# Three more tiles turned by VectorE, gather slots cleared later, result adds and scatters later, in a masked-attention kernel

## The chip, the cores and the metric

The kernel runs on one core of a Trainium2 chip. The metric is the device time of one execution in microseconds (us). Engines: PE is TensorE (matmuls), ACT is ScalarE, DVE is VectorE, POOL is GpSimd, SP is SyncE (it only issues transfers here). Each engine works through its own queue in order; what it issues to the DMA queues runs beside it.

## The reference

The inputs are x (2708 rows of 1024 numbers), a sparse 0/1 matrix adj (2708 x 2708, about four ones to a row), and three weight matrices with biases. What is computed:

```
h = max(layernorm(x), 0)
q, k, v = h @ Wq.T + bq,  h @ Wk.T + bk,  h @ Wv.T + bv
z = (q @ k.T) / 32 * adj;  zeros of z become -10000
out = x + relu(softmax(z, axis=1) @ v)
```

## The kernel before

All numbers are 32-bit floats. The rows are 22 tiles of 128 (the last has 20 rows). Because adj is so sparse, the kernel never forms q @ k.T. It multiplies Wq and Wk into one matrix M, searches each row of adj for its ones, sorts the rows by their number of ones (two separate sorts, of the first 8 tiles and of the rest), and then, for each row, gathers only the rows of h that it needs.

**Start.** Up to about 104 us PE forms M, while x is normalised and stored to `h_dram`. The search on DVE (line 389) goes on to 199 us. The second sort, of the first 8 tiles, ends with `pos_i` (line 689). POOL then *puts* (line 626) the list of each row into a table in memory at its sorted place, and the table is loaded back (`reload`). From then on POOL can gather.

**Units.** From 106 us PE works through 20 units of two tiles each, numbered n = 0 to 19, and then one single tile. Units 0 to 9 ("q") multiply pairs of h tiles by M. Units 10 to 19 ("o") multiply pairs of attention sums by Wv. The pairs of the last units are 18 = (14, 1), 19 = (16, 9); the single tile is 8. A unit is a two-by-two block product done with seven blocks of eight matmuls instead of eight blocks (Winograd's form), so sums and differences of operands (line 722, on DVE) go in, and sums of results (lines 1091, 1094, 1121, 1125 or 1152, 1156) come out. `multiply` (from line 1044) walks through a unit in seven steps i = 0 to 6, calling `after(i)` at each, where everything else is placed. The first two blocks of the next unit (`between`, `opened`) run ahead of the last block of this one; for unit 19 the single tile's first block (`one_started`) takes that place.

**Turning.** A block needs its left operand transposed. There are two ways. *Turned* (`half_turned`, line 415): PE transposes 128 x 128 pieces against an identity matrix, eight to a tile, and ACT copies them out of PSUM (line 718, or 422 for the single tile). *Faced* (lines 695 to 706 and 942 to 946): ACT copies the finished sums `u` into another order `v` (line 944) and stores them to `u_dram` (line 946); four loads (`by_quarters`, line 700, issued by SP) bring the tile back with its 32 x 32 squares in their places; DVE transposes within the squares (`faces`, line 705). The upper half of the next unit's operands is made at step 0, the lower half at step 2. Of the o tiles, those of units 10 to 14 are faced. The later ones are turned; seven of those, the last pair and the single one among them, stay in SBUF (`held`) and go to PE directly.

**The stream.** From unit 4 on, the attention itself runs on DVE as one stream of steps, tile after tile in the list `order`, which ends with 14, 1, 16, 9, 8: *scores* (line 863, one op for each gathered row), *weights* (lines 906 to 912) and *sums* (lines 923 and 929). `advance(share)` at each step of a unit lets as much of the stream into DVE's queue as `share` (line 1233) allows, 20.9 us a unit, less 2.3 for each faced tile of the next unit. DVE keeps this written order. POOL gathers rows of h into 11 slots (line 610). A gather leaves out the lists' empty places, so the slots are cleared once beforehand: eight on DVE (line 1254, in program order at step 1 of unit 4) and three on POOL in quarters (line 1304, behind the counts of the sort).

**Results.** In an o unit, ACT writes relu of the four results into `ya` and `yb` (lines 1118, 1122, 1126, 1134), four such buffers in all. POOL then adds the rows of x to each by an accumulating gather (`add_x`, line 1109), and scatters the previous one to the output (`scatter`, line 808). The last unit (`ends`, line 1140) gathers its x rows beforehand (line 612), and DVE adds (line 1146). The last tile of 20 rows, all equal, is made from one row (`tail`, line 1175) during unit 14.

Of the kernel before, what the change touches and what calls it, by code (L numbers as in the profile page):

```python
# [18 lines left out]
P = 128  # L19
# [46 lines left out]
def tile_preln_masked_attention(  # L66
# [852 lines left out]
    def sums(t):  # L919
        u, coef, m = us.pop(t)  # L920
        for s in range(0 if t in EMPTY else 1, K[t]):
            fill()
            chained(lambda: nc.vector.scalar_tensor_tensor(  # L923
                u, g_of[t][s], coef[:, s:s + 1], u, op0=ALU.mult, op1=ALU.add))
            free.append(g_of[t][s])
            yield 1.3
        fill()
        if t in HOSTS:
            chained(lambda: nc.vector.scalar_tensor_tensor(
                u[:HP], g_of[t][K[t]][:HP], m[:HP, 3:4], u[:HP], op0=ALU.mult, op1=ALU.add))  # L930
            free.append(g_of[t][K[t]])
            yield 1.3
            fill()
        g_of.pop(t)
        if t == SECOND:
            nc.sync.dma_start(v_dram, u)
            whole_second.append(True)
            return
        unit = next((n for n, pair in enumerate(units) if pair[0] == "o" and t in pair[1:]), len(units))
        if now < [unit - 2, 2] and unit <= len(q_pairs) + 4:  # L940
            faced_tiles.add(t)
        if t in faced_tiles:
            v = row_tile(f"v_{t}")
            nc.scalar.copy(v.rearrange("p (a c r) -> p c a r", a=QUADS, r=QP),
                           u.rearrange("p (c a r) -> p c a r", a=QUADS, r=QP))
            nc.scalar.dma_start(u_dram[t * P:(t + 1) * P, :], v)
        elif near(t):
            held[t] = u
        else:
            nc.sync.dma_start(u_dram[t * P:(t + 1) * P, :], u)  # L950
        done.add(t)
# [159 lines left out]
    def o_results(ta, tb):  # L1111
        ya = work.tile([P, D], FT, tag="q", name=f"y_{ta}", bufs=4)
        yb = work.tile([P, D], FT, tag="q", name=f"y_{tb}", bufs=4)
        if (ta, tb) == o_pairs[-1]:
            return ends(ya, ta, yb, tb)

        def c11(X):
            nc.scalar.activation(ya[:, lo], X, AF.Relu)

        def c22(Y, p5):  # L1120
            nc.vector.tensor_add(p5, copied(Y), p5)
            nc.scalar.activation(yb[:, hi], p5, AF.Relu)

        def c12(Z, u2):
            nc.vector.tensor_add(u2, Z, u2)
            nc.scalar.activation(ya[:, hi], u2, AF.Relu)
            if ta == NT - 2:

                nc.sync.dma_start(tail_dram, ya[P - 1:, :])
            send(add_x(ya, ta))  # L1130
            sent.append((ya, ta))

        def c21(Y):
            nc.scalar.activation(yb[:, lo], Y, AF.Relu)  # L1134
            send(add_x(yb, tb))
            sent.append((yb, tb))

        return c11, c22, c12, c21

# [23 lines left out]

        return c11, c22, c12, c21

    sent = []

    def send(behind):

        while sent:  # L1170
            y, t = sent.pop(0)
            with tc.issue_after(behind.ins):
                scatter(y, t, P)

    def tail(t):
        n = tiles[t][1]
        y = work.tile([P, D], FT, tag="q", name=f"y_{t}", bufs=4)
        nc.sync.dma_start(y[:n], tail_dram.to_broadcast([n, D]))
        add_x(y, t, n)
        scatter(y, t, n)  # L1180

    def of_wv(i, j):

# [41 lines left out]
    for n, unit in enumerate(units):  # L1225
# [4 lines left out]
            ordered.enter_context(tc.manual_schedule(engines={mybir.EngineType.DVE}))  # L1230
            nc.sync.dma_start(bp_dram, bp_sb[0:1, :])
        turn = n in (0, FIRST - 1)
        share = 20.9 / 7
        nxt = units[n + 1] if n + 1 < len(units) else None
        if nxt is not None and nxt[0] == "o":
            share -= 2.3 / 7 * len(set(nxt[1:]) & faced_tiles)
# [1 line left out]

        def after(i):
            now[1] = i  # L1240
            if (n, i) in steps_ahead:
                follow(steps_ahead[n, i])
            if (n, i) == (2, 5):
                owe(8)
                owe(9)
                rows_of[FIRST] = load_rows(units[FIRST])
                owe(10)
                owe(6)
                owe(7)
                rows_of[FIRST + 1] = load_rows(units[FIRST + 1])  # L1250
                pooled.close()
            if (n, i) == (FIRST, 1):
                for g in slots[:HIGH - 3]:
                    nc.vector.memset(g, 0.0)
            b11, b12, b21, b22 = M[:, 0, 0], M[:, 0, 1], M[:, 1, 0], M[:, 1, 1]
            for at, place, src in (((-1, 0), b12, of_wv(0, 1)), ((0, 0), b11, of_wv(0, 0)), ((0, 2), T[:, 1], of_wv(1, 1)),
                                   ((0, 3), b21, of_wv(1, 0)), ((0, 4), b22, of_wv(1, 1))):
                if (n - last_q, i) == at:
                    nc.sync.dma_start(place, src)
            for at, place, a, b in (((0, 2), T[:, 0], b12, b11), ((0, 4), T[:, 1], T[:, 1], T[:, 0]),  # L1260
                                    ((1, 0), T[:, 2], b22, b12), ((1, 1), T[:, 3], b21, T[:, 1])):
                if (n - last_q, i) == at:
                    nc.vector.tensor_sub(place, a, b)
            if (n - last_q, i) == (1, 1):
                free.extend(M.rearrange("p i j (a c) w -> p i j a (c w)", a=2)[:, 0, 1, a, :] for a in range(2))
            if (n, i) == (FIRST, 5):
                next(stream)
            if (n, i) == (FIRST, 6):
                chain.append(behind[-1])
                next(stream)  # L1270
                nc.vector.tensor_tensor(bad, bad, total, op=ALU.not_equal)
            if (n, i) == (FIRST + 1, 6):
                marked(EARLY, NT)
            if (n, i) == (FIRST + 2, 4):
                nc.vector.tensor_scalar(msq, msq, MLIMIT, None, op0=ALU.is_gt)
            if n > FIRST + 1 or n == FIRST + 1 and i > 1:
                advance(share)
            if nxt is not None:

                if i == (3 if n == 0 else 4 if turn else 0):  # L1280
                    ops_of[n + 1] = blocks(*rows_of[n + 1], nc.gpsimd if n + 1 < FIRST - 1 else None)
                    with tc.issue_after(products[-1].ins) if n + 1 == FIRST else nullcontext():
                        ops_of[n + 1][1]()
                if i == (4 if n == 0 else 5 if turn else 2):
                    ops_of[n + 1][2]()
                    rows_of.pop(n + 1)
                    if n == last_q - 1:
                        all_rows()
                if i == 3:
                    banks_of[n + 1] = banks_for(bp_sb)  # L1290
                if i == 6 and n + 2 < FIRST:
                    natural_rows(n + 2)
                if i == (2 if n in (FIRST, last_q) else 4) and n + 2 > FIRST and n + 2 < len(units) and n + 2 not in rows_of:
                    while units[n + 2][0] == "o" and not done.issuperset(units[n + 2][1:]):
                        advance(1.0)
                    rows_of[n + 2] = load_rows(units[n + 2])
            if (n, i) in steps_at:
                follow(steps_at[n, i])
            if (n, i) == (3, 4):
                searched()  # L1300
            if (n, i) == (3, 5):
                for s in range(8, HIGH):
                    for c in range(0, D, D // 4):
                        clear = nc.gpsimd.memset(slots[s][:, c:c + D // 4], 0.0)
                        tc.add_manual_dep(clear.ins, counted_at[-1].ins.name,
                                          mybir.DependencyInfo(mybir.DependencyClass.Sync, mybir.DependencyReason.DATA),
                                          reason="not beside the counts")
            if i == 3 and units[n - 1][0] == "o" and NT - 2 in units[n - 1][1:]:
                tail(NT - 1)
            if nxt is None and i == 1:  # L1310
                while alone not in done:
                    advance(1.0)
                r, = load_rows(("o", alone))
                single["turned"] = turned(r, "alone")
            if nxt is None and i == 3:
                single["banks"] = banks_for(bp_sb)
            if n == last_q - 1 and i == 4:

                nc.sync.dma_start(bp_sb, bv.to_broadcast([P, D]))
            if (n, i) == (last_q, 1):  # L1320
                nc.vector.tensor_sub(bp_sb[:, NB:], bp_sb[:, NB:], bp_sb[:, :NB])
# [233 lines left out]
```

## Time and profile before

| what | value |
|---|---|
| median of 3 runs | 639.91 us (639.73 to 640.34) |
| the profiled execution | 639.94 us |
| its span, first to last instruction | 638.1 us |
| PE clock granted | 0.997 of full speed |
| PE, DVE, ACT, POOL busy | 98%, 82%, 44%, 56% of the span |
| memory moved by DMA | 176.96 MB, mean 277 GB/s |

The span is what the trace covers; 1.84 us of the execution lie around it. A matmul's recorded duration reaches past the start of the next one, so the cost of an item on PE is read from start to start. "Idle before, releaser" in a row says how long the engine stood before it and what ended that.

### The profile page before, as it was taken

How to read it: one execution, taken by the hardware profiler on the slowest of the kernel's cores; microseconds unless marked ns; L12 is line 12 of the kernel's file. 1: busy time of each engine (PE TensorE's matmuls, PEld its weight loads, DVE VectorE, ACT ScalarE, POOL GpSimd, SP SyncE). 2: the span in 40 equal slices, each digit the busy share in tenths (PEclk: the TensorE clock that was granted, in tenths of full speed). 3: DMA queues.
4: the chain of work that ended last, by engine and by line, in shares of the span. 5: the costliest groups of instructions: out<-in, count | busy, mean ns of one | idle time of the engine just before them, and what ended most of it. 6: DMA issues, size and time to landing. Idle time of an engine off the chain costs nothing.

```text
span 638.1 us, 6156 instructions
## 1 busy us (share of the span) xinstructions
PE 627.8 (98%) x1651; PEld 317.9 (50%) x1651; DVE 522.4 (82%) x1016; ACT 283.6 (44%) x423; POOL 360.2 (56%) x383
## 2 busy tenths in 40 slices
PE   9999999999999999999999999999999999999994
PEld 5777766444444444444444444444444444444441
DVE  5999888997997625999888999999999889989121
ACT  3538985849667533424342144343342432333200
POOL 2639960885768357565651663476466878633311
PEclk9999999999999999999999999999999999999998
DMA  8999997598796439996798998999999999853631
GB/s 335 407 362 321 342 351 286 200 323 330 255 379 231 171 95 317 327 323 223 233 299 289 290 414 222 295 344 311 363 382 325 325 290 291 266 145 77 187 119 50
DMA packets 60192, 176.96 MB, mean 277 GB/s; under 512 B 9799, under 2 KB 15255, under 8 KB 59512
## 3 DMA queue, kind: packets, MB, share of 16 engines
q0 software_dynamic: 25136, 78.41, 39.4%
q1 hardware_dynamic: 29514, 78.61, 35.0%
q10 hardware_dynamic: 5502, 19.48, 7.8%
q8 instruction: 15, 0.25, 0.2%
q14 instruction: 25, 0.20, 0.1%
HBM read 145.65 MB, written 40.74 MB: 292 GB/s over the span
## 4 chain that ended last, share of the span: by engine, by line
PE 90%; issue 4%; POOL 2%; DMA 2%; DVE 1%; POOLq 0%; ACT 0%; ACTq 0%; DVEq 0%
PE ps L1010 40%; PE psy L1010 29%; PE ps_y L476 6%; PE ps_x L476 4%; PE ps_z L476 4%; PE pt L415 4%; POOL g L610 2%; DMA v_dram<-u 1%; DMA M<-h_dram,tab 1%; PE ps_y L511 1%; DVE junk L863 0%; PE ps_h L1218 0%; PE ps_v L594 0%; DVE u L923 0%; DVE s L722 0%
## 5 line engine op out<-in xcount | busy, mean ns | idle before, releaser
L610 POOL DMA_INDIRECT g<-h_dram,tab x94 | 120.2, 1278 | 79.9 <-DVE u L923 30.0
L1010 PE MATMUL psy<-wlow,s 128*128 128x512 f32 x320 | 144.0, 592 | 0.0
L1010 PE MATMUL ps<-M,a 128*128 128x512 f32 x320 | 144.0, 593 | 0.0
L863 DVE SCALAR_TENSOR_TENSOR junk<-g,pq 128x1024 uint8<-128x1024 f32 x93 | 113.8, 1224 | 13.4 <-DMA g<-h_dram,tab 10.4
L1010 PEld LDWEIGHTS ps<-M,a 128*128 128x128 f32 x320 | 59.7, 190 | 70.4 <-issue 69.1
L923 DVE SCALAR_TENSOR_TENSOR u<-g,coef,u 128x1024 f32<-128x1024 f32 x69 | 88.4, 1281 | 7.0 <-ACT u L912 5.8
L1010 PEld LDWEIGHTS psy<-wlow,s 128*128 128x128 f32 x320 | 59.6, 190 | 69.2 <-issue 69.0
L389 DVE FIND_INDEX8 at<-ones,adj 128x8 uint32<-128x685 f32 (+1 forms) x88 | 74.5, 864 | 0.0
L1010 PE MATMUL ps<-wlow,s 128*128 128x512 f32 x160 | 72.0, 593 | 0.4 <-DVE s L722 0.4
L1010 PE MATMUL ps<-M,s 128*128 128x512 f32 x160 | 72.1, 592 | 0.0
L1010 PE MATMUL psy<-wlow,a 128*128 128x512 f32 x160 | 72.0, 593 | 0.0
L368 ACT ACTIVATE sized<-adj 128x2708 uint8<-128x2708 f32 (+1 forms) x22 | 54.3, 2467 | 7.4 <-DMA adj<-in_adj_dram 6.1
L298 POOL TENSOR_TENSOR hsum<-hsum,x 128x256 f32<-128x256 f32 (+1 forms) x56 | 38.6, 732 | 26.2 <-DVE wlow L444 22.5
L1109 POOL DMA_INDIRECT y<-in_x_dram,tab x19 | 34.2, 1798 | 28.9 <-ACT y L1134 12.1
L1010 PEld LDWEIGHTS ps<-wlow,s 128*128 128x128 f32 x160 | 30.3, 190 | 38.9 <-issue 38.5
L1010 PEld LDWEIGHTS psy<-wlow,a 128*128 128x128 f32 x160 | 30.3, 190 | 38.5 <-issue 37.3
L1010 PEld LDWEIGHTS ps<-M,s 128*128 128x128 f32 x160 | 30.3, 190 | 38.1 <-issue 37.4
L808 POOL DMA_INDIRECT out_dram<-y,tab x21 | 27.4, 1306 | 32.0 <-DMA y<-in_x_dram,tab 15.8
L912 ACT ACTIVATE u<-g,coef 128x1024 f32<-128x1024 f32 x18 | 20.7, 1149 | 35.8 <-DVE coef L911 35.6
L276 ACT ACTIVATE x<-x,r 128x1024 f32<-128x1024 f32 (+1 forms) x22 | 25.9, 1232 | 6.6 <-POOL r L266 6.6
L722 DVE TENSOR_TENSOR s<-a,pt 128x512 f32<-128x512 f32 x30 | 19.2, 681 | 10.9 <-ACT a L718 10.9
L476 PE MATMUL ps_y<-wlow 128*128 128x512 f32 x64 | 27.6, 592 | 0.0
(251 smaller groups left out, 843.3 us busy)
## 6 DMA issues: line engine op xcount, KB each, us to landing
adj<-in_adj_dram SPq DMA_DIRECT2D x21, 1354.0 KB, 11.5
x<-in_x_dram SPq DMA_DIRECT2D x21, 512.0 KB, 8.2
h_dram<-x ACTq DMA_DIRECT2D x21, 512.0 KB, 7.4
q_late<-q SPq DMA_DIRECT2D x12, 512.0 KB, 5.1
pq<-q_late SPq DMA_DIRECT2D x12, 512.0 KB, 6.6
u_dram<-v ACTq DMA_DIRECT2D x10, 512.0 KB, 6.4
or<-u_dram SPq DMA_DIRECT2D x40, 128.0 KB, 7.0
M<-in_wv_dram SPq DMA_DIRECT2D x4, 1024.0 KB, 8.4
```

What stands on the lines that cost most here:

```text
L276: nc.scalar.activation(xs[i][:n], xs[i][:n], AF.Relu, bias=r[:n, 4, i:i + 1], scale=r[:n, 3, i:i + 1])
L298: small.append(nc.gpsimd.tensor_add(hsum[:n, cols], hsum[:n, cols], xt[:n, cols]))
L368: nc.scalar.activation(sized[:n], a[:n, :, :PW], AF.Abs, accum_out=total[:n, t:t + 1])
L389: nc.vector.max_index(at[:n, k - first_k, g, :], ones[:n, 0:8], a[:n, g, :])
L415: nc.tensor.transpose(pt[:, c, :], xt[:, k * P:(k + 1) * P], ident)
L476: mm = nc.tensor.matmul(bank, a_tile(o + H * a[0], a[1], i), b(o), start=first and o == 0, stop=(o == H - 1), skip_group_check=True)
L610: return nc.gpsimd.indirect_dma_start(out=dst, out_offset=None, in_=src, in_offset=off, bounds_check=N - 1, oob_is_err=False)
L808: to = nc.gpsimd.indirect_dma_start(out=out, out_offset=bass.IndirectOffsetOnAxis(ap=ptab.bitcast(U32)[:n, t, SLOTS:SLOTS + 1], axis=0), i ...
L863: chained(lambda: nc.vector.scalar_tensor_tensor(junk, g_of[t][s], 1.0, tq[t], op0=ALU.mult, op1=ALU.mult, accum_out=zall[:, t, s:s + 1]))
L923: chained(lambda: nc.vector.scalar_tensor_tensor(u, g_of[t][s], coef[:, s:s + 1], u, op0=ALU.mult, op1=ALU.add))
L1010: mm = nc.tensor.matmul(bank, a[:, c, :], b[:, c, :], start=False, stop=(c == 3), skip_group_check=True)
L1109: return nc.gpsimd.indirect_dma_start(out=y[:n], out_offset=None, in_=x, in_offset=off, compute_op=ALU.add)
```

## The change

There are five edits. (a) The condition for a faced tile now also takes the last pair (16, 9) and the single tile 8. The single tile's sums have to be in the stream by step 6 of unit 18, where its loads are issued, and `faces` transposes it on DVE at step 1 of unit 19. (b) The stream's budget is 21.5 us in units 15 to 19. (c) DVE's eight clears are queued behind the second sort, four at step 1, two at step 4 and two at step 5 of unit 4; POOL's clears behind the last put. (d) The adds of x are issued at later steps, through the list `due`, and each scatter follows one add later than before. (e) The 20-row tail takes a tile of the row ring, and its scatter goes through the common list.

The diff, without a line that prints during the build:

```
-        if now < [unit - 2, 2] and unit <= len(q_pairs) + 4:
+        if now < [unit - 2, 2] and unit <= len(q_pairs) + 4 or unit >= len(units) - 1:
             faced_tiles.add(t)
...
         def c12(Z, u2):
...
-            send(add_x(ya, ta))
-            sent.append((ya, ta))
+            due.append((now[0], 5, ya, ta))
 
         def c21(Y):
             nc.scalar.activation(yb[:, lo], Y, AF.Relu)
-            send(add_x(yb, tb))
-            sent.append((yb, tb))
+            due.append((now[0] + 1, 1, yb, tb))
...
-    sent = []
-
-    def send(behind):
-
-        while sent:
-            y, t = sent.pop(0)
+    sent, due = [], []
+
+    def add_due():
+
+        while due and due[0][:2] <= tuple(now):
+            y, t = due.pop(0)[2:]
+            send(add_x(y, t), 1)
+            sent.append((y, t, P))
+
+    def send(behind, stay=0):
+
+        while len(sent) > stay:
             with tc.issue_after(behind.ins):
-                scatter(y, t, P)
+                scatter(*sent.pop(0))
 
     def tail(t):
         n = tiles[t][1]
-        y = work.tile([P, D], FT, tag="q", name=f"y_{t}", bufs=4)
+        y = row_tile(f"y_{t}")
         nc.sync.dma_start(y[:n], tail_dram.to_broadcast([n, D]))
         add_x(y, t, n)
-        scatter(y, t, n)
+        sent.insert(0, (y, t, n))
...
-        share = 20.9 / 7
+        share = (20.9 if n < len(units) - 5 else 21.5) / 7
...
         def after(i):
             now[1] = i
+            add_due()
...
-            if (n, i) == (FIRST, 1):
-                for g in slots[:HIGH - 3]:
-                    nc.vector.memset(g, 0.0)
+            if n == FIRST and i in (1, 4, 5):
+                for g in slots[:4] if i == 1 else slots[4:6] if i == 4 else slots[6:8]:
+                    with tc.issue_after(sorted_at[-1].ins):
+                        nc.vector.memset(g, 0.0)
...
-            if (n, i) == (3, 5):
+            if (n, i) == (3, 6):
                 for s in range(8, HIGH):
                     for c in range(0, D, D // 4):
-                        clear = nc.gpsimd.memset(slots[s][:, c:c + D // 4], 0.0)
-                        tc.add_manual_dep(clear.ins, counted_at[-1].ins.name,
-                                          mybir.DependencyInfo(mybir.DependencyClass.Sync, mybir.DependencyReason.DATA),
-                                          reason="not beside the counts")
+                        with tc.issue_after(entered[-1].ins):
+                            nc.gpsimd.memset(slots[s][:, c:c + D // 4], 0.0)
...
             if nxt is None and i == 1:
+                uT = work.tile([P, D], FT, tag="hT", name="T_alone", bufs=2).rearrange("p (c q) -> p c q", q=P)
+                faces(uT, single["rows"], 0, DC)
+                single["turned"] = uT
+            if n == len(units) - 2 and i == 6:
                 while alone not in done:
                     advance(1.0)
-                r, = load_rows(("o", alone))
-                single["turned"] = turned(r, "alone")
+                single["rows"], = load_rows(("o", alone))
```

More of the change, by code (lines that the diff above doesn't have):

```diff
@@ L939, in sums @@
         unit = next((n for n, pair in enumerate(units) if pair[0] == "o" and t in pair[1:]), len(units))
-        if now < [unit - 2, 2] and unit <= len(q_pairs) + 4:
+        if now < [unit - 2, 2] and unit <= len(q_pairs) + 4 or unit >= len(units) - 1:
             faced_tiles.add(t)
+        print("done", t, "at", now, "unit", unit, t in faced_tiles)
         if t in faced_tiles:
```

## The prediction

> **What bounds the kernel now.** I read the page first, then who TensorE (PE) waits for, then the last 90 us engine by engine. The page's head, and its DMA busy shares by slice (40 slices of 16 us, in tenths):
>
> ```profile
> span 638.1 us, 6156 instructions
> ...
> PE 627.8 (98%) x1651; PEld 317.9 (50%) x1651; DVE 522.4 (82%) x1016; ACT 283.6 (44%) x423; POOL 360.2 (56%) x383
> ...
> DMA  8999997598796439996798998999999999853631
> ```
>
> The waits of PE, all there are in the whole span (us in total, times, longest):
>
> ```profile
> PE ps_y L511 <- POOL hsum L121: 1.2, 1, 1.2
> PE ps L1010 <- DVE s L722: 0.4, 1, 0.4
> ```
>
> PE is the bound from its first matmul to its last: it waits 1.6 us in 638. So an edit gains only what it takes off PE's own queue, or off what follows PE's last matmul, and it loses only where it makes PE wait. PE's queue at the end, unit 18 from 571.43 and unit 19 from 597.21 (start, duration, line, output<-inputs):
>
> ```profile
> 571.43 1.04 PE L415 MATMUL pt<-ident,u 128*128 128x128 f32 x8
> 572.30 3.60 PE L1010 MATMUL psy<-wlow,s 128*128 128x512 f32 x8
> 575.74 1.04 PE L415 MATMUL pt<-ident,u 128*128 128x128 f32 x8
> 576.61 3.60 PE L1010 MATMUL ps<-M,a 128*128 128x512 f32 x8
> ...
> 597.21 1.04 PE L415 MATMUL pt<-ident,u 128*128 128x128 f32 x8
> 598.09 3.60 PE L1010 MATMUL psy<-wlow,s 128*128 128x512 f32 x8
> ...
> 608.39 3.60 PE L1010 MATMUL psy<-wlow,s 128*128 128x512 f32 x8
> 611.82 3.60 PE L1010 MATMUL ps<-M,T_alone 128*128 128x512 f32 x8
> ```
>
> The three groups of line 415 turn tiles 16 and 9 (the last pair) and 8 (the single tile). From start to start, which is what an item costs in a pipelined queue, one takes 572.30 - 571.43 = 0.87, 576.61 - 575.74 = 0.87 and 598.09 - 597.21 = 0.88 us, and a block of eight matmuls 3.43 to 3.44.
>
> **The change part by part.**
>
> (1) *Three tiles turned by VectorE (DVE).* The three groups leave PE: **-2.62 us**, if what replaces them is in time. What replaces each: a copy on ScalarE (ACT, line 944), a store (946), four loads (700), transposes on DVE (705). From the views of those lines:
>
> ```profile
> L944 ACT COPY v<-u x10: 1044/1045/1052, 262.4 to 419.2; 128x1024 f32<-128x1024 f32 x10
> ```
>
> ```profile
> DMA to landing us min/median/max: 6.1/6.4/6.9
> ```
>
> ```profile
> L700 SPq DMA_DIRECT2D or<-u_dram x40: 302/430/672, 322.8 to 437.3; - x40
> ...
> DMA to landing us min/median/max: 3.0/7.0/15.1
> ```
>
> ```profile
> L705 DVE STREAM_TRANSPOSE a<-or x15: 668/704/711, 345.1 to 452.6; 128x512 f32<-128x512 f32 x15
> L705 DVE STREAM_TRANSPOSE s<-or x5: 664/669/672, 355.8 to 453.2; 128x512 f32<-128x512 f32 x5
> ```
>
> The first landing row is that of the stores. A turned tile thus takes 1.05 + 6.4 + 3 x 0.43 (the fourth load is issued that much after the first) + 7.0 = 15.7 us by medians (10.4 and 24.3 by the ends) to reach DVE, and DVE about 1.3 more (two of 0.65, since such ops start a little before their predecessor's recorded end). The copy replaces two copies of ACT out of PSUM, of about the same length. Now the DVE rows around these tiles:
>
> ```profile
> 558.72 2.60 DVE L923 SCALAR_TENSOR_TENSOR u<-g,coef,u 128x1024 f32<-128x1024 f32 x2
> ...
> 570.58 1.22 DVE L863 SCALAR_TENSOR_TENSOR junk<-g,pq 128x1024 uint8<-128x1024 f32 x1
> ...
> 574.59 5.25 DVE L923 SCALAR_TENSOR_TENSOR u<-g,coef,u 128x1024 f32<-128x1024 f32 x4 [1.66 <-ACT u L912]
> 579.75 1.28 DVE L722 TENSOR_TENSOR s<-a,pt 128x512 f32<-128x512 f32 x2
> ...
> 584.79 0.68 DVE L1125 TENSOR_TENSOR u<-ps,u 128x512 f32<-128x512 f32 x1
> 585.39 1.27 DVE L923 SCALAR_TENSOR_TENSOR u<-g,coef,u 128x1024 f32<-128x1024 f32 x1
> 586.70 1.28 DVE L929 SCALAR_TENSOR_TENSOR u<-g,m,u 64x1024 f32<-64x1024 f32 x1
> ...
> 612.02 0.69 DVE L1152 TENSOR_TENSOR p<-psy,p 128x512 f32<-128x512 f32 x1 [1.94 <-PE psy L1010]
> ```
>
> Tile 9's sums end at 561.2 (first row). With 15.7 us its rows are there at 576.9; unit 18's lower half, now line 722 at 579.75, asks for them no sooner, so about 3 us are spare, and tile 16, done some 12 us before it, has more. PE needs those operands late: unit 19 is opened only behind unit 18's fourth block.
>
> Tile 8 is the tight one. I count the steps in the new order, with the budget of line 1233 spent as before: the last score ends at 571.8; the two transposes of tile 16 add 1.3 (573.1); weights and ACT's first product take what they take now, 574.59 - 571.8 = 2.8 (575.9); three sums 3.9 (579.8); the lower half 1.3 + 2.5 (583.6); two sums 2.6, line 1125 0.6, two sums 2.6 (589.4); line 1121, which the smaller share of unit 18 puts ahead of the last sum, 0.6; line 929 1.2. It ends at **591.2**, where it ends at 587.9 now. Copy 592.4, store landed 598.8, fourth load issued 600.1, landed 607.1, transposed **608.4**. All of that is an estimate from the rows above. PE asks for it at the single tile's first block: 611.82 - 2.62 = **609.2**. So by medians it fits with 0.8 us to spare. Those medians are from busy stretches; this stretch is lighter (the page's slices from 590 to 622 have DMA busy shares of 0.6 and 0.3, those from 383 to 447, where most loads of line 700 ran, 0.8 or 0.9), so I take 4 to 6 for the last load and a spare of 2 to 4 us. The ends: 603.1 with 6.1 and 3.0, and 617.0 with 6.9 and 15.1. Behind the waiting transposes stand, on DVE, unit 19's evictions: lines 1146, 1156 and 1152. PE waits for 1152 alone, before unit 19's last block at 609.2 + 3.4 = 612.6; behind the transposes it needs three ops of 0.6 to 0.7 and its own, so 608.4 + 2.7 = 611.1: covered as long as the single tile's own block is.
>
> [...]
>
> (2) *The early clears.* Before: eight on DVE, twelve on POOL, all ahead of the first put.
>
> ```profile
> 219.82 0.17 DVE L689 CAST pos_i<-deg 128x8 uint32<-128x8 f32 x1
> 224.75 1.28 DVE L722 TENSOR_TENSOR s<-a,pt 128x512 f32<-128x512 f32 x2 [4.75 <-ACT a L718]
> ...
> 241.99 1.23 DVE L863 SCALAR_TENSOR_TENSOR junk<-g,pq 128x1024 uint8<-128x1024 f32 x1 [7.25 <-DMA g<-h_dram,tab]
> ...
> 249.55 1.28 DVE L722 TENSOR_TENSOR s<-a,pt 128x512 f32<-128x512 f32 x2 [3.70 <-ACT a L718]
> ```
>
> ```profile
> L1254 DVE MEMSET g<- x8: 912/912/912, 201.9 to 212.6; 128x1024 f32 x8
> ```
>
> ```profile
> 217.37 3.13 POOL L1304 MEMSET g<- 128x256 f32 x12 [9.82 <-ACT q L1099]
> 220.68 1.02 POOL L626 DMA_INDIRECT tab_dram<-tab,pos_i  x1 [0.18 <-issue]
> ...
> 235.20 0.98 POOL L612 DMA_INDIRECT pq<-q_dram,tab  x1 [4.45 <-DMA tab<-tab_dram]
> ```
>
> Sorting, puts and first gathers start earlier, by 0.5 us (POOL's clears alone) to 4 or 5 (with the four clears that lie inside the sort). The first score at 241.99 comes earlier by as much; then DVE waits at 249.55 for PE's turned tile, 3.70 us now and the gain more afterwards. So it is worth **0**. The moved clears fit into idle time: four of 0.91 to 1.07 us into the 4.75 before 224.75, twelve in 3.13 into POOL's 4.45 before 235.20, the other four into the 7.25. If that cover fails, up to 4 us go into DVE's slack, not to PE. PE's 0.4 us wait (at 389) I leave as it is; bounds -0.4 to +0.5.
>
> (3) *Adds and scatters later.* Landing times of the scatters (808) and adds (1109):
>
> ```profile
> DMA to landing us min/median/max: 3.3/6.5/11.5
> ```
>
> ```profile
> DMA to landing us min/median/max: 6.2/8.7/14.8
> ```
>
> ```profile
> 580.25 0.60 ACT L1118 ACTIVATE y<-ps 128x512 f32<-128x512 f32 x1 [3.23 <-PE ps L1010]
> ...
> 589.11 0.63 ACT L1122 ACTIVATE y<-p 128x512 f32<-128x512 f32 x1 [1.41 <-DVE p L1121]
> ```
>
> A scatter now goes out one add later, so POOL seldom stands before an add's landing and gathers queued behind get earlier. The price: of four result buffers, each is held longer. The first tile's scatter leaves some 17 us into the next unit and lands near 25; its buffer is written 25.8 + 8.8 = 34.6 in (580.25 - 571.43 = 8.8): 10 spare. The second's leaves about 5 into the unit that reuses it, lands near 12.5, and is written 17.7 in: 5 spare, none with the slowest landing (11.5), and then ACT still has some 6 us before PE needs its next copy. **0** for PE; bounds 0 to +3 over the run. In unit 19 the two gathers of x wait for buffers and come about 7 us later, still before DVE, held by tile 8, asks for them.
>
> (4) *Tail row tile, pacing.* 21.5 for 20.9 in units 15 to 17 moves three ops of each behind stream work by at most 1.8 us, against 10 us of slack; no instruction is added. **0**. What follows the last matmul is untouched:
>
> ```profile
> 629.41 0.69 DVE L1371 SCALAR_TENSOR_TENSOR y_alone<-ps,y_alone 128x512 f32<-128x512 f32 x1 [1.95 <-PE ps L1010]
> ```
>
> from there to the end are 8.7 us of eviction, scatter and closing.
>
> Sum: span 638.1 - 2.62 = 635.5. The profiled execution took 639.94 in all, 1.84 around its span, and lies 0.03 above the median of 639.91. So 639.94 - 2.62 = **637.3 us**. A measurement of this kernel tells about 0.2% from no change: faster is below 638.6, slower above 641.2.
>
> **Rivals.**
>
> *A. Tile 8's rows come late* (the side of slower). For: only 0.8 us spare by medians, DMA on every leg, and scatters, adds and gathers of x now leave in the same 15 us. Against: lighter DMA. Every us behind 609.2 is one of PE's: even at 611.8, slower from there, and beyond 0.2% from 613.1. With the slowest leg of each kind, 617.0 - 609.2 = 7.8, so 645.1. Chance 0.28: 0.08 below 638.6, 0.12 within, 0.08 slower.
>
> *B. DVE becomes the bound*, the turning itself is paid: +1.3, 641.2. [...] Speaks against it: PE waits for DVE 0.4 us in the whole span, and DVE's last rows above have idle time before them. Chance 0.03, within.
>
> *C. A result buffer is held too long*, ACT stands before line 1122 in units 11 to 16, where DMA is busiest, and PE behind it: say 1 us in each of six, 643.3. Chance 0.05.
>
> *D. The transposes go and the time doesn't*: the queue before them was hiding waits of the next block, so PE waits 2 us of the 2.62 for its copies: 639.3. Against: unit 18 takes 597.21 - 571.43 = 25.78; less two groups of 0.87 that is 24.04, just seven blocks of 3.43, so nothing waits beneath them. Chance 0.04.
>
> **How the numbers follow.** The forecast, 637.3 with its own range 636.7 to 637.9, gets 0.60. Faster 0.60 + 0.08 = 0.68; within 0.12 + 0.03 + 0.04 = 0.19; slower 0.08 + 0.05 = 0.13. The range goes from 636.6 (PE's 0.4 us gone too) up into A, to 640.8, and leaves out about 0.15.
>
> **What would show it.** Right: line 415 has 24 fewer matmuls from u; units 18 and 19 take 24.0 us each; PE's waits stay under 2 us in all; the single tile's transposes end before its first block; the first score comes sooner, the wait at 249.55 is longer. Wrong: PE waiting on T_alone or on line 1152 (A), PE waiting on line 722 in units 16 to 18 (B), ACT standing before a y for a scatter (C).

## The result, and the profile after

The changed kernel takes 638.23 us (median of 10 executions, 636.89 to 639.76), the kernel before, on the same chip, 640.16 (10, 639.63 to 642.51). The medians lie 1.93 us apart. The ratio over all executions is 0.9966, with a 95% interval of 0.9954 to 0.9978, which is about 2.2 us less. The prediction's 637.3 against its base of 639.91 is a ratio of 0.9959. The profiled execution took 638.00, 1.94 less than the one of before. From line 941 to 1128, line numbers are one higher in the changed kernel's profile (1010 is 1011, 1091 is 1092, 1109 is 1110); behind that they shift otherwise (1146 is 1145).

The head of the page after, with the row of DMA busy shares:

```profile
span 636.3 us, 6139 instructions
...
PE 624.6 (98%) x1627; PEld 315.5 (50%) x1627; DVE 525.7 (83%) x1021; ACT 283.5 (45%) x421; POOL 361.8 (57%) x383
...
DMA  8998897598696439986699998999999999893761
```

PE has 24 matmuls and 3.2 us of work less, VectorE (DVE) 3.3 us more. All waits of PE in the span:

```profile
PE psy L1011 <- DVE q L1092: 1.4, 1, 1.4
PE ps_y L511 <- POOL hsum L121: 1.2, 1, 1.2
```

The 0.4 us wait for line 722 is replaced by one of 1.4 for the line that forms q, so PE's waits add up to 2.6 us and not 1.6. First the end, PE's timeline (start, duration, what it does):

```profile
571.92 3.60 PE L1011 MATMUL psy<-wlow,s 128*128 128x512 f32 x8
...
595.95 3.60 PE L1011 MATMUL psy<-wlow,s 128*128 128x512 f32 x8
...
609.69 2.74 PE L1011 MATMUL ps<-M,T_alone 128*128 128x512 f32 x6
```

Unit 18 takes 595.95 - 571.92 = 24.03 us, seven blocks of 3.43, where it took 25.78. No transposes stand between the blocks, and the single tile's first block (its row is cut by the window's edge) has no wait. DVE in the same stretch:

```profile
591.14 1.27 DVE L929 SCALAR_TENSOR_TENSOR u<-g,m,u 64x1024 f32<-64x1024 f32 x1
...
605.03 1.25 DVE L705 STREAM_TRANSPOSE T_alone<-or 128x1024 f32<-128x1024 f32 x1 [11.56 <-DMA or<-u_dram]
...
627.28 0.69 DVE L1379 SCALAR_TENSOR_TENSOR y_alone<-ps,y_alone 128x512 f32<-128x512 f32 x1 [1.95 <-PE ps L1011]
```

Tile 8's sums end at 591.14 + 1.27 = 592.4. Its rows are turned at 605.03 + 1.25 = 606.3, 3.4 us before PE asks at 609.69. The DVE row in the middle carries the whole trip: DVE stands 11.56 us for the loads from u_dram.

Then the middle. PE, after:

```profile
368.81 3.70 PE L1011 MATMUL psy<-wlow,a 128*128 128x512 f32 x8 [1.41 <-DVE q L1092]
372.35 3.60 PE L1011 MATMUL psy<-wlow,s 128*128 128x512 f32 x8
...
389.74 3.67 PE L1011 MATMUL ps<-wlow,s 128*128 128x512 f32 x8
```

The last row is the block that waited 0.36 us before the change, where it began at 389.03. It begins 0.71 later now. From that block to the end of the span are 638.1 - 389.03 = 249.07 us before and 636.3 - 389.74 = 246.56 after: the end gives 2.51, and the part ahead of it takes 0.71 back. DVE after, in the part ahead:

```profile
240.41 1.22 DVE L863 SCALAR_TENSOR_TENSOR junk<-g,pq 128x1024 uint8<-128x1024 f32 x1 [5.10 <-DMA g<-h_dram,tab]
...
247.40 1.28 DVE L722 TENSOR_TENSOR s<-a,pt 128x512 f32<-128x512 f32 x2 [3.23 <-ACT a L718]
...
293.68 1.23 DVE L863 SCALAR_TENSOR_TENSOR junk<-g,pq 128x1024 uint8<-128x1024 f32 x1 [3.10 <-DMA g<-h_dram,tab]
295.85 1.23 DVE L863 SCALAR_TENSOR_TENSOR junk<-g,pq 128x1024 uint8<-128x1024 f32 x1 [0.94 <-DMA g<-h_dram,tab]
```

The first score comes 1.58 us sooner than before (241.99) and the turned tile 2.15 sooner (249.55), with a wait that is shorter, not longer. Near 294 DVE then stands 4.04 us for gathers (the last two rows), where it stood 0.84 before:

```profile
291.28 1.23 DVE L863 SCALAR_TENSOR_TENSOR junk<-g,pq 128x1024 uint8<-128x1024 f32 x1 [0.24 <-DMA g<-h_dram,tab]
...
292.91 1.22 DVE L863 SCALAR_TENSOR_TENSOR junk<-g,pq 128x1024 uint8<-128x1024 f32 x1 [0.39 <-DMA g<-h_dram,tab]
...
294.35 1.23 DVE L863 SCALAR_TENSOR_TENSOR junk<-g,pq 128x1024 uint8<-128x1024 f32 x1 [0.21 <-DMA g<-h_dram,tab]
```

### The profile page after: what moved, and what is told of

Its sections match the earlier page's. It is cut to its first block, busy times and chain, and to the rows that moved or that the text cites. A ratio compares the mean times of both kernels' runs of the same rounds, so it can differ in the third digit from the quotient of the medians.

```text
span 636.3 us, 6139 instructions
## 1 busy us (share of the span) xinstructions
PE 624.6 (98%) x1627; PEld 315.5 (50%) x1627; DVE 525.7 (83%) x1021; ACT 283.5 (45%) x421; POOL 361.8 (57%) x383
## 4 chain that ended last, share of the span: by engine, by line
PE 85%; DVE 6%; issue 4%; DMA 3%; SPq 1%; POOL 0%; ACT 0%; POOLq 0%; DVEq 0%; ACTq 0%
PE ps L1011 38%; PE psy L1011 28%; PE ps_y L476 6%; PE ps_x L476 4%; PE ps_z L476 4%; PE pt L415 3%; DVE u L923 2%; DMA g<-h_dram,tab 1%; DMA or<-u_dram 1%; DVE junk L863 1%; DVE s L722 1%; DVE wlow L1270 1%; PE ps_y L511 1%; SPq L700 1%; DVE q L1092 0%
## 5 line engine op out<-in xcount | busy, mean ns | idle before, releaser
L808 POOL DMA_INDIRECT out_dram<-y,tab x21 | 25.0, 1188 | 16.4 <-DVE flag L1354 6.1
L626 POOL DMA_INDIRECT tab_dram<-tab,pos_i x22 | 21.9, 995 | 20.7 <-DVE pos_i L689 15.3
L760 ACT COPY ps<-bp_sb 128x512 f32<-128x512 f32 x42 | 24.5, 595 | 7.2 <-DVE y L1145 6.7
```

Source lines behind the costliest of these rows:

```text
L760: nc.scalar.copy(return_[h], row[:, h * NB:(h + 1) * NB])
L808: to = nc.gpsimd.indirect_dma_start(out=out, out_offset=bass.IndirectOffsetOnAxis(ap=ptab.bitcast(U32)[:n, t, SLOTS:SLOTS + 1], axis=0), i ...
```

## The experiments

The theory after the result: the tail gives its 2.6 us, and the moved clears cost the 0.7 in the middle. Rivals: the 0.7 is scatter in when gathers land; and the moved adds and scatters, priced at 0, are needed to have tile 8's rows in time. Each ratio is against the kernel before on the same chip in the same session. Kernels changed from the kernel before have its line numbers; so, up to line 1128, have those changed from the changed kernel, which lack its one printing line.

### The three parts alone

**Tail alone**: the kernel before with

```
-        if now < [unit - 2, 2] and unit <= len(q_pairs) + 4:
+        if now < [unit - 2, 2] and unit <= len(q_pairs) + 4 or unit >= len(units) - 1:
...
-        share = 20.9 / 7
+        share = (20.9 if n < len(units) - 5 else 21.5) / 7
```

and the single tile's loads and transposes as in the changed kernel.

> Only the last pair and the single tile are turned by VectorE, with the 21.5 us budget; clears, adds and scatters as before. Theory 1 (the tail gives all of 2.6 us and the rest was lost in the middle by the earlier clears): 640.0 - 2.6 = 637.4, PE's wait near 389 about 0.4 us as before. Rival 2 (the loss in the middle is scatter between runs in when a gather near 290 lands, whatever edit is made): also about -2.6 in the tail, but with a middle that is 0 to 1 us later here too, 637.4 to 638.4. Rival 3 (the adds and scatters took part of the gain, and are needed to get the tiles in time): the single tile's first block waits for its transposes, and the time is 638 to 640.

**Clears alone**: the kernel before with the two edits of the clears, those of (FIRST, 1) and (3, 5).

> Only the clears are moved, behind the sort on VectorE and behind the puts on GpSimd. Theory 1 (moved clears cost the middle): 640.0 + 0.7 to 1.0 = 640.7 to 641.0, with PE waiting over 1 us near 368 or 389. Rival 2 (scatter between runs): 640.0 within 0.5, PE waits near 389 between 0 and 1.5 us. As the prediction had it (worth nothing): 640.0.

**Adds and scatters alone**: the kernel before with due, add_due, the scatter one add later and the last rows' row tile.

> Only the adds of x, the scatters and the 20-row tail are moved. Nothing of them runs before 390 us. All theories: 640.0 within 0.4; rival 3 (they matter for the tail) would show only together with the turned tiles. If results are held too long, PE waits in units 12 to 18 and the time is above 641.

**All but the clears**: the changed kernel with the clears of the kernel before.

> The changed kernel with the clears put back where they were. Theory 1 (clears cost the middle): 0.7 to 1.0 us faster than the changed kernel's 638.2, so 637.3. Rival 2 (scatter): the same as the changed kernel within 0.4, so 637.8 to 638.6.

```
                     median   ratio    95% interval
tail alone           640.80   0.9994   0.9976 to 1.0012
clears alone         640.93   1.0004   0.9995 to 1.0012
adds and scatters    640.50   1.0001   0.9991 to 1.0011
all but the clears   637.94   0.9957   0.9942 to 0.9973
```

No part alone has a gain clear of noise; the tail and the adds together give the whole gain. That the moved clears cost the 0.7 is not borne out: with the old clears back the time is 637.94, where that theory had 637.3, and the clears alone are equal to the kernel before of their own session (640.64).

The twelve executions of the tail alone run from 638.05 to 644.39. Three took 638.05 to 638.21, like the changed kernel, so the gain is there at times. The trace is of one of the longer ones, 642.58, and shows what goes wrong there. First PE's waits, then PE's and DVE's timelines, then the row of ten us in the view by windows (the last three numbers are the granted clock, the DMA engines' busy share and GB/s):

```profile
PE ps L1010 <- DVE T_alone L705: 2.8, 1, 2.8
PE ps_y L511 <- POOL hsum L121: 1.2, 1, 1.2
PE ps L1010 <- DVE s L722: 0.8, 1, 0.8
```

```profile
612.51 5.40 PE L1010 MATMUL ps<-M,T_alone 128*128 128x512 f32 x8 [2.84 <-DVE T_alone L705]
617.74 3.60 PE L1010 MATMUL psy<-wlow,a 128*128 128x512 f32 x8
```

```profile
593.23 1.27 DVE L929 SCALAR_TENSOR_TENSOR u<-g,m,u 64x1024 f32<-64x1024 f32 x1
...
611.21 1.25 DVE L705 STREAM_TRANSPOSE T_alone<-or 128x1024 f32<-128x1024 f32 x1 [15.64 <-DMA or<-u_dram]
```

```profile
612.00:622.00 10.00, 9.49 (x20) 4.33 (x21) 6.25 (x14) 1.18 (x2) 0.96 (x1) 0.83 0.31 107
```

This is rival A of the prediction. Tile 8's sums start 2.1 us later than in the changed kernel, its trip through DRAM (start of line 929 to start of the transpose) takes 611.21 - 593.23 = 18.0 us and not 13.9, and PE stands 2.84 us: the 2.1 and the 4.1 together, less the 3.4 that the changed kernel has to spare. Where the 2.1 come from was not tested; from 495 to 540 us DVE stood 5.8 us for gathered rows here, 2.8 in the changed kernel and 2.7 in the kernel before. The block behind the wait then takes 617.74 - 612.51 = 5.23 us from start to start and not 3.43: 4.6 us lost in all, more than the 2.6 won.

What differs beside the trip stands on GpSimd's (POOL's) queue. Its gathers of x for the last pair, in the tail alone and then in the changed kernel:

```profile
594.49 0.97 POOL L612 DMA_INDIRECT y<-in_x_dram,tab  x1 [0.30 <-issue]
599.12 0.94 POOL L612 DMA_INDIRECT y<-in_x_dram,tab  x1 [3.65 <-DMA out_dram<-y,tab]
```

```profile
596.77 0.97 POOL L612 DMA_INDIRECT y<-in_x_dram,tab  x1 [4.69 <-DMA out_dram<-y,tab]
...
604.76 0.99 POOL L612 DMA_INDIRECT y<-in_x_dram,tab  x1 [2.58 <-DMA out_dram<-y,tab]
```

In the tail alone both gathers run beside tile 8's store (issued at 595.61) and its loads (601.81); in the changed kernel the second comes after most of the loads' time. The loads' time to landing, tail alone and changed kernel (count, KB each, us; the trace has the landing of one of the four):

```profile
or<-u_dram SPq DMA_DIRECT2D x4, 128.0 KB, 8.5
```

```profile
or<-u_dram SPq DMA_DIRECT2D x4, 128.0 KB, 4.7
```

From the first load's issue to the transpose are 9.4 us in the tail alone and 7.2 in the changed kernel (597.81 to 605.03); from the store's issue to the first load, 6.2 and 4.3. The DMA engines' busy share does not tell the two apart: it is 0.85 from 602 to 612 us in the tail alone and 0.92 from 597.81 to 605.03 in the changed kernel, so the loads are slower where the share is lower. What goes with the trip's length is the place of the two gathers. That they lengthen it is argued, not shown, as no run moves them alone and other adds and scatters move with them.

### Which half of the adds' edit: scatters one add later, adds where they were

The changed kernel again, and from it (f3_scatter_later):

```
-            due.append((now[0], 5, ya, ta))
+            send(add_x(ya, ta), 1)
+            sent.append((ya, ta, P))
```

and the same for yb.

> The changed kernel again, as an anchor for the three beside it. About 2 us below the kernel before (ratio 0.996 to 0.998). In its trace: the block behind the single tile's row transpose begins without a wait; the block at 389 to 390 us (behind the operand s of L722) begins 0.3 to 1.0 us later than in the kernel before (389.03) if the moved clears are what delays the middle, and anywhere from 388.5 to 390 if it is where the gathers land.

> The changed kernel with the adds of x issued where they were (as the results are done), and only the scatters one add behind. In the tail edit alone GpSimd waited 13.8 us for its adds to land ahead of scatters, and in the changed kernel 2.8 us. If that wait is what delayed the late tiles (theory), moving the scatters alone keeps it short: GpSimd's wait at the scatter stays under 5 us, tile 8's sums end within 1 us of the changed kernel's, PE has no wait at the single tile's block, and the time is within 0.4 us of the changed kernel. If the place of the adds matters (rival: their packets on the DMA engines beside the gathers), tile 8's sums end 1 to 2 us later, PE waits 1 us or more at the single tile's block, and the time is 1 to 3 us above the changed kernel.

Measured: the changed kernel again 637.89, ratio 0.9962 (0.9948 to 0.9977); scatters later alone 637.83, 0.9955 (0.9942 to 0.9968). The place of the adds does nothing; what is left of the edit counts, the scatters' place and the last rows' row tile together. POOL's waits at line 808 for an add to land, 390 to 600 us, for the kernel before, the tail alone, and scatters later:

```profile
POOL out_dram L808 <- DMA y<-in_x_dram,tab: 12.2, 4, 5.3
```

```profile
POOL out_dram L808 <- DMA y<-in_x_dram,tab: 13.8, 4, 4.8
```

```profile
POOL out_dram L808 <- DMA y<-in_x_dram,tab: 2.8, 1, 2.8
```

PE has no wait at the single tile's block here.

### The tail and the late scatters without the row tile; the row tile without the late scatters

Both are the tail alone with one more edit. In g_min the four results' scatters go one add later and the last 20 rows keep one of the four result buffers (tag q); in h_last_rows only the buffer changes:

```
 g_min
-            send(add_x(ya, ta))
+            send(add_x(ya, ta), 1)
 h_last_rows
-        y = work.tile([P, D], FT, tag="q", name=f"y_{t}", bufs=4)
+        y = row_tile(f"y_{t}")
```

> The kernel before with the tail edit and one more: each scatter goes out behind the next tile's add of x and not behind its own (clears, adds and the last row tile as before). If the scatters' place is all that tile 8 needs (theory): GpSimd's wait at the scatters is under 5 us, PE has no wait at the single tile's block, and the time is within 0.5 us of the changed kernel, 2.2 to 3 us below the kernel before. If the moved adds or the row tile for the last rows are needed too (rival): a wait of over 1 us at the single tile's block and a time within 1 us of the tail edit alone.

> The kernel before with the tail edit and one more: the last 20 rows' result stands in a row tile instead of the fourth result buffer; adds, scatters and clears as before, so that GpSimd still waits 12 to 14 us for its adds ahead of the scatters. If those waits make tile 8 late (theory): the time stays within 1 us of the tail edit alone (2 to 3 us above the changed kernel), tile 8's sums end 2 us or more later than in the changed kernel (591.1), and PE waits over 1 us at the single tile's block. If it is the result buffer that the last rows take (rival): sums end near 591, no such wait, and the time is within 0.7 us of the changed kernel.

Measured for g_min: 644.21, ratio 1.0070 (1.0057 to 1.0083), **slower** than the kernel before (640.03) by 4.2 us, which neither reading had. Its timelines of POOL, ACT and PE:

```profile
491.17 1.88 POOL L1109 DMA_INDIRECT y<-in_x_dram,tab  x1 [7.17 <-DMA y<-tail_dram]
```

```profile
503.45 0.63 ACT L1122 ACTIVATE y<-p 128x512 f32<-128x512 f32 x1 [14.63 <-DMA out_dram<-y,tab]
```

```profile
505.64 3.70 PE L1010 MATMUL ps<-M,s 128*128 128x512 f32 x8 [1.95 <-ACT p L1026]
```

With scatters late, a result buffer is held longer; the last rows take one of the four, POOL stands 7.17 us for their load with the held scatters queued behind it, ACT stands 14.63 us before it may write the next result, and PE 1.95 behind ACT. This is rival C's mechanism, at one place. Four shorter waits of PE follow, 0.36 to 1.15 us, so that it stands 4.9 us in all behind 500 us, and loses more than the three transposes give. Tile 8's trip is 14.0 us here too (599.75 to 613.78), but all that leads to it is late. The versions with late scatters that do gain have the edit to the last rows, which the prediction passed over at 0: their row tile, with their own scatter behind the next one's add. So that edit is what makes the late scatters affordable; its two halves weren't tried one without the other.

Measured for h_last_rows: 648.12, ratio 1.0064 (1.0029 to 1.0100); this chip takes 643.61 for the kernel before, so the ratio is what counts, and the profiled execution is a long one (651.18). The trip takes 18.1 us (600.64 to 618.73), POOL waits 13.7 at line 808, and PE:

```profile
373.61 5.17 PE L1010 MATMUL psy<-wlow,a 128*128 128x512 f32 x8 [3.27 <-DVE q L1091]
...
620.03 6.54 PE L1010 MATMUL ps<-M,T_alone 128*128 128x512 f32 x8 [4.16 <-DVE T_alone L705]
626.41 3.60 PE L1010 MATMUL psy<-wlow,a 128*128 128x512 f32 x8
```

The row tile without the late scatters does not help tile 8. Over all runs with tile 8 on that trip, it takes 13.5 to 14.4 us in the eight whose scatters go one add later, and 18.0 and 18.1 in the two whose scatters don't. In the changed kernel and in all but the clears, the two gathers of x leave 3.25 and 3.50, then 11.24 and 11.64 us behind the store's issue; in the two, 1.1 ahead of it and 3.5 behind.

### The last pair without the single tile

The changed kernel with `unit == len(units) - 1` in the condition, and the single tile turned by PE as before.

> The changed kernel with only the last output pair turned by VectorE: the single tile's rows are kept in SBUF and turned by PE as in the kernel before. If each group of transposes is worth its own PE time, 0.88 us above the changed kernel, and no wait for the single tile's rows in the trace. If the single tile's trip through DRAM costs PE anything in the changed kernel, less than 0.5 us above or even below it.

Measured: 639.14, ratio 0.9979 (0.9970 to 0.9988), 1.25 us above the changed kernel (637.89) in the same session, against 0.88 for the one group. No row waits for tile 8. The profiled run's block near 389 us began at 390.43, the latest of those that carry the moved clears, so the odd 0.4 is of the size of the middle's scatter. So nothing shows that tile 8's trip costs the changed kernel anything.

### The middle: more room ahead of 389 us

The changed kernel with the old clears, and 2.6 us of the gather stream taken from unit 9; given back in unit 11 (f1_gate) or in unit 10 (g_gate10):

```
+        share += {last_q: -2.6 / 7, last_q + 2: 2.6 / 7}.get(n, 0.0)
```

> The changed kernel with the clears where they were, and with 2.6 us of VectorE's gather stream moved from the unit ahead of the first output unit to two units later. If the middle is set by VectorE's arrival at 368 and 389 us (theory), PE's waits there (1.4 and about 0.4 to 0.7 us) go, the block behind operand s begins at 388.3 to 388.7, and the time is 0.4 to 1.4 us below the changed kernel. If the waits there are only a place where an earlier lag shows (rival: the lag returns at a later operand because the stream is then behind), the waits go at 389 and come back between 390 and 560 us, and the time is within 0.4 us of the changed kernel.

> As the gate version before (clears as they were, 2.6 us of VectorE's gather stream moved behind the operands of 389 us), but the stream is made up within the next unit and not two units later, so that the first output pair's adds and scatters find the gathers ahead of them on GpSimd where they were. If it was the late first scatter (421.3 against 417.8 us) that held ScalarE and cost 5 us (theory): first scatter before 419 us, ScalarE's wait for a result buffer near 430 us under 3 us, no wait of PE there, and 0.3 to 1 us below the changed kernel. If the stream has no room at all after 390 us (rival): a wait of PE over 1 us somewhere between 390 and 560 us, and a time 1 us or more above the changed kernel.

Measured for f1_gate: 641.36, ratio 1.0018 (1.0003 to 1.0033), 3.5 us slower than the changed kernel. The waits at 368 and 389 are gone, and the block near 389 begins at 388.02, but the first scatter now leaves at 421.30 (417.78 with the same clears and the old budget), as it stands on POOL behind gathers that wait for the stream's buffers (3.03 us at 405.85, 6.33 at 415.39). The chain is short, ACT first, then PE:

```profile
430.68 0.60 ACT L1118 ACTIVATE y<-ps 128x512 f32<-128x512 f32 x1 [5.14 <-DMA out_dram<-y,tab]
```

```profile
432.47 5.18 PE L1010 MATMUL psy<-wlow,s 128*128 128x512 f32 x8 [3.08 <-ACT u L1054]
437.49 3.60 PE L1010 MATMUL ps<-M,a 128*128 128x512 f32 x8
```

3.08 us of waiting and 1.6 for the slower block behind it (5.02 us from start to start for 3.43). A lag that comes back later is the rival's, but it comes by a result buffer, not by the operand that the rival named, and it costs 3.5 us where the rival had at most 0.4.

Measured for g_gate10: 639.74, ratio 0.9991 (0.9970 to 1.0012), from 636.82 to 646.23: the least sure time of all versions. Its profiled execution is one of the long ones. The first scatter left at 421.99, not before 419, and ACT stood 8.23 us before the result that it lets through; then PE waited for DVE, which had stood 7.20 us for a row of pq:

```profile
439.50 1.23 DVE L863 SCALAR_TENSOR_TENSOR junk<-g,pq 128x1024 uint8<-128x1024 f32 x1 [7.20 <-DMA pq<-q_late]
```

```profile
442.82 6.58 PE L1010 MATMUL ps<-wlow,s 128*128 128x512 f32 x8 [4.28 <-DVE s L722]
449.24 3.60 PE L1010 MATMUL psy<-wlow,a 128*128 128x512 f32 x8
```

So the rival's two signs came, a wait over 1 us and a time 1.6 us above the 638.10 of g_late in the same session (below; it counts as a run of the changed kernel). The theory's condition, a first scatter before 419, was not met, so it was not tested. Why that row of pq came so late, and what the execution of 636.82 did otherwise, stays open: the trace is of a long one alone.

### Tile 8 later on purpose

The changed kernel with the single tile's loads (they are four, of 128 KB) and transposes one place later, the loads named to be issued after a block of PE.

> The changed kernel with the single tile's 12 row loads issued only after PE has done the block behind the s2 operand of the last output pair, some 4 to 6 us later than 593.5 us, and VectorE's transposes of them one place later. The changed kernel has 3.4 us to spare between the single tile's last transpose (606.2) and its first block (609.7). By the prediction's rule each us past 609.2 is one of PE's: with loads 4 to 6 us later, a wait of 0.6 to 2.6 us and the same on the time. By the tail edit's run (rival) a wait of 2 to 3 us costs PE about 1.8 us more, by a lower granted clock behind it: a wait of 2 us or more gives a time 3.5 us or more above the changed kernel, with a granted clock under 0.9 in the 10 us behind the wait. A wait under 1.5 us costs only itself.

Measured: 638.10, ratio 0.9965 (0.9953 to 0.9978). The edit does not do what it was meant to: naming a block of PE did not hold back the loads, which SP issues, and they left at 596.9 as in the changed kernel (596.7 in its second profile). It says nothing on the price of a wait, and counts as one more run of the changed kernel.

### The moved clears over all runs

The clears' worth is read from every profile but those with a changed budget and h_last_rows, whose chip is 3 us behind the others: the first score's start, DVE's waits for gathered rows (g, pq, M) from 250 to 390 us, and the start of PE's block near 389.

```
                     first score  waits  block near 389
clears as before
  before             241.99       2.0    389.03
  tail alone         241.88       3.0    389.29
  adds, scatters     241.54       3.2    389.41
  all but clears     241.70       1.5    389.03
  g_min              242.54       3.7    390.08
clears moved
  changed            240.41       5.1    389.74
  changed again      240.50       4.8    389.08
  scatters later     240.84       5.2    389.51
  pair only          241.18       4.5    390.43
  g_late             240.97       2.1    389.38
  clears alone       240.87       5.7    389.99
```

On the means, the moved clears start the stream 1.1 us sooner (240.80 against 241.93), and DVE waits 1.9 us longer for rows (4.6 against 2.7). The block comes at 389.69 against 389.37, but the two groups overlap from 389.1 to 390.1. The head start is given back at the gathers. Whether 0.3 us more is lost, the runs don't settle.

## Why the prediction was right, and where it was not

**Three transposes off PE, -2.62**: right. From the block near 389 to the end it is -2.51 in the trace; units 18 and 19 lost just the groups, so rival D is out. DVE took 1.25 us for tile 8 (line 705), where a group took PE 0.88; this cost nothing, as PE's one wait for DVE, 1.41 us at 368.81, is ahead of all three tiles. No run shows rival B's +1.3 as a price: it is the author's estimate, three tiles of 1.3 us on DVE less the 2.62 of PE.

**Tile 8 in time**: right for this kernel, but not for the reason given. The sums end 1.2 us later than worked out (592.4 for 591.2), and the one load whose landing is known took 4.7 us, where 4 to 6 was taken: turned at 606.3 for 608.4, asked for at 609.7. The 4 to 6 were taken because the stretch is light on DMA (shares of 0.6 and 0.3 before). It isn't in the changed kernel (a share of 0.92 from the first load's issue to the transpose), and in the tail alone, at 0.85, a load took 8.5. That the spare held was in part luck. Two ends of the working are also 1.0 too early by their own terms: 10.4 for the trip should be 11.4, and 603.1 should be 604.1; nothing else hangs on them.

**"0 for PE" for the late adds and scatters**: the step that failed. Alone they are worth 0 (1.0001), but the tail's 2.62 hangs on them: without them the same tail gives 0.9994. So the sum has the right number for a change whose parts depend on each other in a way that it did not see. The prediction did note that the two gathers of x "come about 7 us later", and put it down as harmless; by the traces that shift goes with a trip of 13.5 to 14.4 us in place of 18. It also passed over a price: without the edit to the last rows, taken at 0 with the pacing, the late scatters left the kernel 4.2 us slower than before.

**"Every us behind 609.2 is one of PE's"**: too small a price. 2.84 us of lateness cost 4.6 in the tail alone. Rival A's scale, "slower from 611.8", should have begun between 611.2 and 611.8, an estimate from the blocks behind waits: 0.1 us slower behind 1.95, 1.8 behind 2.84.

**Early clears, 0, with the wait at 389 left as it is, bounds -0.4 to +0.5**: right on the worth, too narrow on the bounds. The block moved by +0.71 in the profiled run and by +0.05 to +1.40 in the others with moved clears. The gap between 637.3 and 638.23 is of this size. The reason given, that the gain would show as a longer wait at 249.55, was wrong: the wait is shorter (3.23), the gain passes it and is lost near 294. Of the signs of being right, this one failed, and so did PE's waits under 2 us in all (2.6).

**Rivals**: A and C both came true, not in the changed kernel but in kernels with fewer of the edits: A in the tail alone, C in g_min.

None of the versions tried is surely faster than the changed kernel; scatters later alone (0.9955) and all but the clears (0.9957) are equal to it within their intervals, with less of the edit.

## What to carry to other kernels

Work taken off the bounding engine is won only if what replaces it arrives in time, so list which transfers run beside that trip, and don't go by the DMA engines' busy share alone: here the loads were slower where the share was lower (8.5 us at 0.85, 4.7 at 0.92). An edit that looks like housekeeping (when a scatter leaves, which buffers a small tile sits in) may be what pays for it. Price parts of a change in pairs as well as alone; here no part alone has a gain clear of noise, and one pair is worth it all. Read the spread of a version's executions too: the tail alone has the full gain in three of twelve. Moving work from one place with little spare to the next can move the wait and make it longer: in f1_gate the waits at 368 and 389 us went, and one of 3.08 came at 432.

## What the runs showed of the hardware

In these runs a wait of up to 1.95 us cost PE 0.1 us more than itself, and one of 2.84 or more made the next block much slower too. Blocks of eight behind a wait, by their recorded length (3.60 without a wait): 3.67 to 3.70 behind waits of 0.36 to 1.95 us, 5.40, 5.18 and 5.17 behind 2.84, 3.08 and 3.27, and 6.54 and 6.58 behind 4.16 and 4.28. So the extra cost was 1.6 to 3.0 us in these five cases; no block behind a wait between 1.95 and 2.84 us was measured. The granted clock was 0.83 over ten us behind the wait of 2.84 (tail alone, 612 to 622) and 1.00 behind the one of 1.41 (changed kernel, 369 to 379). Over the whole profiled execution it was 0.997 in g_min, whose longest wait is 1.95, 0.995 in the changed kernel and in the tail alone, 0.993 in f1_gate (3.08), 0.991 in g_gate10 (4.28) and 0.987 in h_last_rows (3.27 and 4.16).
